# Queries in the rows' product, one gate product of 128 rows, and joined normalisations in a graph-attention kernel

## The chip, the cores and the metric

The kernel runs on one core of a Trainium2 chip. The metric is device time in microseconds for one execution, the median of several runs.

## The reference, cut to what matters

A graph has 6,250 nodes and 200,000 edges sorted by destination. A first network (L0: one attention over the edges and a gate) gives node features of width 64. A second network runs three attention layers with eight heads of eight. One layer, in the reference's words:

```python
h = _ln(x, n1g[l], n1b[l])
q = (h[dst] @ Wq[l] + bq[l]).reshape(-1, H, HD)
kn, ke = h[src] @ Wkn[l] + bkn[l], edge_attr @ Wke[l] + bke[l]     # vn, ve alike
alpha = softmax over the edges of one destination of (q * (kn + ke)).sum(-1) / scale
agg = segment_sum((vn + ve) * alpha, dst)
gate = sigmoid(agg @ Wih[l] + bih[l] + h @ Whh[l] + bhh[l])
upd = agg + gate * (h @ Wself[l] + bself[l] - agg)
x = x + upd @ Wout[l] + bout[l]
x = x + _mlp(_ln(x, n2g[l], n2b[l]), mW1[l], mb1[l], mW2[l], mb2[l])
```

After the third layer x is normalised with a gain and a shift, the input of the three layers is added, and the sum is normalised once more.

## The kernel before

Nodes are sorted by degree into 49 blocks of 128 destinations, one to a partition. All instructions are written out in an order fixed by hand; no scheduler moves them.

**First part, to about 4,850 us.** It sorts, runs L0 over the blocks and computes the edge features (`edge_attr`). Each block ends in `prepare`, described below, which makes what layer 0 needs.

**Layers.** Each of the three layers loops over the blocks in `LORDER` as a pipeline: in iteration i block b is at its keys and values, b1 (the block before) at its softmax and values, b2 at the gate, b3 at the MLP, b4 at preparing the next layer. There are four iterations after the last block, in which the pipeline drains.

- Keys and values of b (`sums`, called once for each group of up to eight edge slots): TensorE multiplies edge features (L1310, float32), then adds rows of neighbours picked by one-hot products. Rows of nodes that stand in the right place come from a table kept in SBUF (L1329, three bfloat16 parts of a row); the others come from rows gathered from HBM (L1317, and L1329 with `g`). ScalarE copies the sums out of PSUM to `b_k` and `b_v` (L1333, L1336). VectorE multiplies `b_k` by the queries and sums over a head (`scores`, L1340 and L1341).
- Gathers: GpSimd issues one indirect DMA per tile of 128 rows (L1239), in bursts of up to twelve into one of four buffers `g`. A burst is issued when TensorE has used the buffer it is to fill.
- Queries of b: one product at the start of the iteration (L1489) into PSUM. The left part of the PSUM tile `b_qe` holds the queries, the right part the exponentials, until the block's values are summed.
- `soft` (L1347 to L1351) and `values` (L1355 to L1380) of b1.
- Small steps of b2, b3, b4 stand in the list `steps` and are put between the groups of b: `turned` transposes the attention of b2 (L559), `gate` multiplies node rows and attention by three matrices (L1390 to L1392; the biases are a 65th row, against a row of ones stored with the node rows `hv`), `gated` mixes on VectorE (L1399 to L1402), `update` multiplies by Wout (L1406, L1407). For b3: `updated` adds and normalises (L1410, `norm`), then `turned2`, `hidden` (L1421) and `close` (L1428 to L1431). In `close`, layers 0 and 1 store x and call `prepare`, which normalises x at once; layer 2 does the two last norms there. For b4 the generator of `prepare` is continued: transpose (L589), the rows' product for keys and values (L601), its copy out (L602) and the split into three bfloat16 parts, stored in the table of the next layer.
- Loads and stores go through the queue of SyncE (SP): node rows and x of the next block at the top of an iteration (`begin`), edge features and one-hots as groups end, stores at the end of an iteration (`flush`).

`norm` is ten VectorE instructions on one block: statistics (L535, L536), variance plus a constant in two scalings (L537), an inverse square root by a bit trick and two Newton steps (`rsqrt`, L519 to L527), and the scaling (L540).


Of the kernel before, what the change touches and what calls it, by code (L numbers as in the profile page):

```python
# [9 lines left out]
F32 = mybir.dt.float32  # L10
# [6 lines left out]
P = 128  # L17
D = 64
# [34 lines left out]
LORDER = (LB, LB - 1) + tuple(b for i in range(24) for b in ((1, 0, *range(2, 24))[i], LB - 2 - i)) [:-1]  # L53
# [371 lines left out]
def passes(ctx, tc, ins, out, meta_d, t0_d, own_d, ident, row_f, ones, norm_c, st_i, id_i, off, end, has, hash_, rdeg,  # L425
# [7 lines left out]
    ht_d = [[dram.tile([D + 1, P], F32, name=f"ht{i}_{b}_d") for b in range(NB)] for i in range(2)]  # L433
    x1_d = [dram.tile([P, D], F32, name=f"x1_{b}_d") for b in range(NB)]
    x2_d = [dram.tile([P, D], F32, name=f"x2_{b}_d") for b in range(NB)]
# [29 lines left out]
    def weights(l):  # L465
# [4 lines left out]
        w["wc"] = wc = lwp.tile([D + 1, 5 * D], F32, name="fwc")  # L470
        bx = lwp.tile([D + 1, 3 * D], F32, name="fbx")
        for i, nm in enumerate(("q", "kn", "vn", "self", "hh")):
            nc.sync.dma_start(wc[:D, i * D : (i + 1) * D], g1("W" + nm))
            nc.sync.dma_start(wc[D : D + 1, i * D : (i + 1) * D], g1("b" + nm).unsqueeze(0))
        for i, nm in enumerate(("ke", "ve", "ih")):
            nc.sync.dma_start(bx[D : D + 1, i * D : (i + 1) * D], g1("b" + nm).unsqueeze(0))
# [4 lines left out]
        w["wih"] = lwp.tile([D, D], F32, name="fwih")  # L481
        nc.sync.dma_start(w["wih"], g1("Wih"))
        w["wout"] = lwp.tile([D, D], F32, name="fwout")
        nc.sync.dma_start(w["wout"], g1("Wout"))
# [17 lines left out]
        nc.vector.tensor_add(wc[D : D + 1, 4 * D :], wc[D : D + 1, 4 * D :], bx[D : D + 1, 2 * D :])  # L502

        nc.vector.tensor_scalar(wc[:, 0:D], wc[:, 0:D], 1.0 / HD ** 0.5, None, ALU.mult)
        nc.vector.tensor_scalar(wc[:, 3 * D : 4 * D], wc[:, 3 * D : 4 * D], 0.5, None, ALU.mult)
# [35 lines left out]

    def norm_twice(wk, once, twice, v):
# [30 lines left out]
    def prepare(wk, mps, w, b, xb, i, hn=None):  # L573
# [9 lines left out]
        kf = wk.tile([P, W1], F32, name="p_kf")  # L583
# [3 lines left out]
        def turned():  # L587
# [4 lines left out]
            stores.append(lambda: nc.sync.dma_start(hd[b][:, :n], ht[:, :n]))  # L592
            if b == 0:
                stores.append(lambda: nc.sync.dma_start(hd[LB][:, LN:P], ht[:, :SPARE]))
# [4 lines left out]
        def rows():  # L599
            pm = mps.tile([P, W1], F32, name="p_pm")  # L600
            nc.tensor.matmul(pm, ht, w["wc"][:, D : 3 * D], start=True, stop=True)  # L601
            nc.scalar.copy(kf, pm)  # L602
            nc.scalar.copy(part[:, 0], kf)
# [1621 lines left out]
```

## Time and profile before

| | |
|---|---|
| runs | 10577.22, 10610.52, 10615.33 us; median 10610.52 |
| profiled execution | 10601.41 us |
| its span, first to last instruction | 10599.5 us |
| mean granted TensorE clock | 0.753 |
| busy: TensorE matmuls, weight loads | 6784.7 us, 4613.5 us |
| busy: VectorE, ScalarE, GpSimd | 5774.5, 3190.8, 3983.4 us |
| gathers of the layers (L1239) | 2,328 in a group of 2245.7 us |
| score products (L1340) | 711 in a group of 542.0 us |

Lines with "PE" are TensorE, "PEld" its weight loads, DVE VectorE, ACT ScalarE, POOL GpSimd. A row of the groups view gives line, engine, operation, output and inputs, shapes and count; then busy time, mean ns of one, and the idle time of the engine before, with what ended it. A row of the timeline gives start, duration, and the instruction; in brackets the idle time of its engine just before and what ended it, where "issue" means that the engine waited for nothing that the trace shows. A row of the waits gives total us, times, longest. A row of busy time by stretch gives the stretch, its length, busy time and count for TensorE matmuls, weight loads, VectorE, ScalarE and GpSimd, then the clock, the DMA engines' share and GB/s.

### The profile page before, as it was taken

To read this page: it belongs to the slowest core of one execution; us is meant where nothing else is said; L and a number is where in the kernel's file an instruction comes from. 1 tells how busy PE (TensorE), PEld (TensorE's weight loads), DVE (VectorE), ACT (ScalarE), POOL (GpSimd) and SP (SyncE) were. 2 spreads that over 40 slices of the span, in tenths; PEclk is the share of its full clock that TensorE was granted. 3 is DMA by queue.
4 is the path that set the end of the run, shared out by engine and by line. 5 is a ranking of instruction groups with operands and counts; after the bars stand their busy time and mean duration, and the time that the engine had idled before them with its cause. 6 is when DMAs were issued, how large, how long until landed. Compare 5 with 4: busy or idle time off the path is not lost.

```text
span 10599.5 us, 163737 instructions
## 1 busy us (share of the span) xinstructions
PE 6784.7 (64%) x62377; PEld 4613.5 (44%) x62377; DVE 5774.5 (54%) x14777; ACT 3190.8 (30%) x6591; POOL 3983.4 (38%) x4201
## 2 busy tenths in 40 slices
PE   2544645555555555576677777677777766677776
PEld 1212222222222222234566666455666655565565
DVE  5544545544555555553556555455665545666666
ACT  1322323322333333342233333223333322222222
POOL 5244333333333333313434444343444434434442
PEclk6676767777777777787787888777778777787877
DMA  4333333333333333334444444444444444444443
GB/s 102 94 89 92 95 89 96 92 90 95 92 91 93 92 91 92 91 87 138 122 128 133 136 136 134 125 123 129 133 134 136 135 130 118 119 126 125 129 127 86
DMA packets 1118549, 1183.96 MB, mean 112 GB/s; under 512 B 669364, under 2 KB 821433, under 8 KB 1110719
## 3 DMA queue, kind: packets, MB, share of 16 engines
q1 hardware_dynamic: 652271, 705.16, 23.3%
q0 software_dynamic: 174624, 393.35, 14.5%
q10 hardware_dynamic: 290864, 74.87, 3.4%
q8 instruction: 502, 8.22, 0.3%
q14 instruction: 288, 2.36, 0.1%
HBM read 936.40 MB, written 236.44 MB: 111 GB/s over the span
## 4 chain that ended last, share of the span: by engine, by line
PE 53%; another core or an unknown queue 19%; issue 17%; ACT 5%; DVE 3%; DMA 1%; POOL 0%; SPq 0%; ACTq 0%; POOLq 0%; DVEq 0%
PE b_pk L1329 18%; PE b_pk L1310 12%; PE f_ph L982 6%; PE b_pk L1317 4%; PE f_tr L945 4%; PE f_pe L964 3%; ACT f_hid L986 2%; ACT s_bc L827 1%; ACT ea L968 1%; PE p_pm L824 1%; ACT f_sq L747 1%; PE p_pm L1421 1%; ACT f_xt L949 1%; PE p_pm L1430 1%
## 5 line engine op out<-in xcount | busy, mean ns | idle before, releaser
L1239 POOL DMA_INDIRECT g<-tab,fidx x2328 | 2245.7, 965 | 3530.2 <-PE b_pk L1317 1720.3
L728 POOL DMA_INDIRECT g<-ft_d,si x1596 | 1522.5, 954 | 2843.0 <-PE e_pt L1045 2370.4
L1329 PE MATMUL b_pk<-ftb,ohl 128*128 128x128 bf16 x21168 | 1889.7, 255 | 881.0 <-issue 830.5
L1329 PEld LDWEIGHTS <-ohl 128*128 128x128 bf16 x21168 | 1592.1, 116 | 1190.5 <-issue 1118.4
L1310 PE MATMUL b_pk<-fwkv,eal 64*128 64x128 f32 x12990 | 1390.8, 316 | 491.0 <-issue 460.2
L1340 DVE TENSOR_TENSOR b_k<-b_k,b_qe 128x768 f32<-128x768 f32 (+6 forms) x711 | 542.0, 762 | 1690.4 <-ACT b_k L1333 1143.9
L964 PE MATMUL f_pe<-f_hid,fw 128*64 128x448 f32 (+4 forms) x2464 | 770.9, 645 | 1080.1 <-ACT ea L968 563.4
L1333 ACT COPY b_k<-b_pk 128x384 f32<-128x384 f32 (+2 forms) x1011 | 475.5, 470 | 3072.4 <-remote 1455.5
L1310 PEld LDWEIGHTS b_pk<-fwkv,eal 64*128 64x128 f32 x12990 | 1064.4, 208 | 719.2 <-issue 634.5
L982 PE MATMUL f_ph<-f_xt,fw 64*128 64x448 f32 (+4 forms) x2464 | 826.1, 678 | 457.8 <-ACT f_xt L949 382.3
L949 ACT ACTIVATE f_xt<-f_tr,feg 128x352 f32<-128x352 f32 (+10 forms) x392 | 253.8, 648 | 2220.2 <-remote 1913.5
L1333 ACT COPY b_v<-b_pk 128x384 f32<-128x384 f32 (+2 forms) x1011 | 872.8, 863 | 0.0
L986 ACT ACTIVATE f_hid<-f_ph,fb 128x448 f32<-128x448 f32 (+4 forms) x1232 | 725.5, 635 | 448.7 <-PE f_ph L982 281.0
L964 PEld LDWEIGHTS f_pe<-f_hid,fw 128*64 128x64 f32 x2464 | 155.1, 149 | 1570.2 <-issue 849.6
L945 PE MATMUL f_tr<-f_mv,f_xs 128*64 128x44 f32 (+10 forms) x12544 | 557.7, 249 | 396.0 <-issue 349.7
L932 DVE TENSOR_TENSOR f_mv<-s_tt,e_fac 128x704 f32<-128x704 f32 (+10 forms) x392 | 349.7, 892 | 778.9 <-remote 663.2
L945 PEld LDWEIGHTS f_tr<-f_mv,f_xs 128*64 128x64 f32 x12544 | 506.3, 160 | 506.1 <-issue 430.4
L982 PEld LDWEIGHTS f_ph<-f_xt,fw 64*128 64x128 f32 x2464 | 261.7, 212 | 822.0 <-ACT f_xt L949 501.2
L1341 DVE TENSOR_REDUCE b_al<-b_k 128x96 f32<-128x768 f32 (+6 forms) x711 | 542.9, 764 | 24.5
L1360 DVE TENSOR_REDUCE b_ag<-b_v 128x64 f32<-128x2816 f32 (+17 forms) x147 | 455.5, 3099 | 5.1
L1359 DVE TENSOR_TENSOR b_v<-b_v,b_qe 128x2816 f32<-128x2816 f32 (+17 forms) x147 | 454.1, 3089 | 0.0
L1317 PE MATMUL b_pk<-g,oh 128*128 128x384 bf16 (+3 forms) x2358 | 446.7, 326 | 0.0
(403 smaller groups left out, 7784.8 us busy)
## 6 DMA issues: line engine op xcount, KB each, us to landing
ohl<-oh_d SPq DMA_DIRECT2D x882, 256.0 KB
eal<-ea_d SPq DMA_DIRECT2D x324, 384.0 KB
oh_d<-s_oh SPq DMA_DIRECT2D x294, 256.0 KB
g<-tab,fidx POOLq DMA_INDIRECT x2328
eal<-ea_d SPq DMA_DIRECT2D x93, 320.0 KB
ea_d<-ea ACTq DMA_DIRECT2D x114, 256.0 KB
eal<-ea_d SPq DMA_DIRECT2D x114, 256.0 KB
ea_d<-ea ACTq DMA_DIRECT2D x130, 224.0 KB
```

The lines of the kernel that those rows point to most:

```text
L728: nc.gpsimd.indirect_dma_start(out=g[:, k - k0, :], out_offset=None, in_=t0_d[:], in_offset=bass.IndirectOffsetOnAxis(ap=got[b]["si"][:, k ...
L945: nc.tensor.matmul(pv[r * D : (r + 1) * D, j], xss[(4 * ORDER.index(b) + 4 * j0 // D) % 4][:, (j0 + j) % (D // 4), :], mv[:, j, :, r::2], ...
L964: nc.tensor.matmul(pe[h * D : (h + 1) * D, :w], w2[:, s, :], hid[s][:, h, :w], start=(s == 0), stop=(s == 1))
L982: nc.tensor.matmul(ph[h][:, :w], w1[r, s * P : (s + 1) * P], xf[r, e0 * D : e1 * D], start=True, stop=True)
L986: nc.scalar.activation(hid[s][:, h, :w], ph[h][:, :w], AF.Relu, bias=b1[:, s : s + 1])
L1239: nc.gpsimd.indirect_dma_start(out=g[:, t - t0, :], out_offset=None, in_=tabs[l % 2][:], in_offset=bass.IndirectOffsetOnAxis(ap=idx[:, f : ...
L1310: nc.tensor.matmul(pk[:, j % 2, j // 2, :], ea[r, e, :], w["wkv"][r], start=(j < 2), stop=False)
L1317: nc.tensor.matmul(pk[:, h, :c, :], ohs[l, b, NW][:, 0, :], rows_[:, slice(t, t + 2 * c - 1, 2), i, :], start=False, stop=(i == 2))
L1329: nc.tensor.matmul(pk[:, h, j, :], o, rows[:, i, :], start=False, stop=(j == c - 1 and q == len(us) - 1 and i == 2))
L1333: nc.scalar.copy(to.rearrange("p (j h) d -> p h j d", h=2), pk[:, :, : n // 2, d0 : d0 + D])
L1340: nc.vector.tensor_tensor(k, k, m["q"].unsqueeze(1).to_broadcast([P, k1 - k0, D]), ALU.mult)
L1341: nc.vector.tensor_reduce(m["al"][:, :, k0:k1].rearrange("p h k -> p k h"), k.rearrange("p k (h d) -> p k h d", h=H), AX.X, ALU.add)
```

## The change

- `prepare` makes queries, keys and values of the next layer in one product of 192 columns and stores the queries beside x (`x1_d`, `x2_d` get 128 columns). `begin` loads both as one tile of SBUF. L1489 goes, and `scores` reads the queries from SBUF instead of PSUM.
- The attention, transposed, is copied to partitions 64 to 127 of the tile whose partitions 0 to 63 are the node rows. One product of 128 rows (Whh over Wih) gives the gate; a second of 64 rows gives Wself. Both outputs lie on PSUM partitions 64 to 127. ScalarE adds the biases: in the Tanh, and in a new Identity that brings the second product to SBUF. VectorE mixes in three instructions instead of four. The row of ones is no longer stored.
- The norm of b3, that of b4 and, in layer 2, the last norm of a fifth block b5 are done together at the top of the iteration (`normed`, `norms`). Before, b3's was there (`updated`) and b4's at the end of `close`. The scaling of layer 2's output is folded into two instructions.
- `steps` has `turned` before b4's transpose, and the gate before b3's transpose.
- `LORDER` begins with four light blocks instead of two, then alternates heavy and light ones as before.

Counted over the program: 294 fewer products on TensorE in the written order, 1,247 fewer instructions on VectorE, 147 more on ScalarE, 150 more DMAs on SP.

```diff
-LORDER = (LB, LB - 1) + tuple(b for i in range(24) for b in ((1, 0, *range(2, 24))[i], LB - 2 - i)) [:-1]
+LORDER = (LB, LB - 1, LB - 2, LB - 3) + tuple(b for i in range(23) for b in ((1, 0, *range(2, 23))[i], LB - 4 - i))[:-1]
...
+    def norms(wk, items):
+
+        k, mvs = len(items), []
+        for v, _ in items:
+            s6 = wk.tile([P, 6], F32, name="n_s6", bufs=4)
+            mvs.append(s6)
+            nc.vector.bn_stats(s6, v)
+        mv = wk.tile([P, k, 2], F32, name=f"n_mv{k}")
+        for j, s6 in enumerate(mvs):
+            nc.vector.bn_aggr(mv[:, j], s6)
+        vv = wk.tile([P, 2, k], F32, name=f"n_vv{k}")
+        for i, f in enumerate((KC, KC * K1 * K1)):
+            nc.vector.tensor_scalar(vv[:, i], mv[:, :, 1], f, f * EPS, ALU.mult, ALU.add)
+        r = rsqrt(wk, vv, k, f"n{k}")
+        for j, (_, put) in enumerate(items):
+            put(mv[:, j, 0:1], r[:, j : j + 1])
...
-            pm = mps.tile([P, W1], F32, name="p_pm")
-            nc.tensor.matmul(pm, ht, w["wc"][:, D : 3 * D], start=True, stop=True)
+            pm = mps.tile([P, 3 * D], F32, name="p_pm")
+            nc.tensor.matmul(pm, ht, w["wc"][:, : 3 * D], start=True, stop=True)
             nc.scalar.copy(kf, pm)
-            nc.scalar.copy(part[:, 0], kf)
+            nc.scalar.copy(part[:, 0], kf[:, D:])
+            stores.append(lambda: nc.sync.dma_start(xd[b][:n, D:], kf[:n, :D]))
...
-            hv = wk.tile([D + 1, P], F32, name="hv", bufs=5)
-            nc.sync.dma_start(hv, ht_d[l % 2][b][:])
-            xb = wk.tile([P, D], F32, name="b_x", bufs=6)
-            nc.sync.dma_start(xb, (x1_d if l == 0 else x2_d)[b][:])
+            hv = wk.tile([P, P], F32, name="hv", bufs=5)
+            nc.sync.dma_start(hv[:D], ht_d[l % 2][b][:])
+            xq = wk.tile([P, 2 * D], F32, name="b_x", bufs=7)
+            nc.sync.dma_start(xq, (x1_d if l == 0 else x2_d)[b][:])
...
-                m["at"] = flip(wk, mps, m["a"], "b_at")
+                pt = mps.tile([D, P], F32, name="p_pm")
+                nc.tensor.transpose(pt, m["a"], ident)
+                nc.scalar.copy(m["hv"][D:], pt)
...
-                nc.tensor.matmul(pg[:, 0], w["wc"][:, 3 * D : 4 * D], hv, start=True, stop=True)
-                nc.tensor.matmul(pg[:, 1], w["wc"][:, 4 * D :], hv, start=True, stop=False)
-                nc.tensor.matmul(pg[:, 1], w["wih"], at, start=False, stop=True)
-                gt = m["gt"] = wk.tile([D, 3, P], F32, name="b_gt")
-                nc.scalar.activation(gt[:, 0], pg[:, 1], AF.Tanh, scale=0.5)
+                nc.tensor.matmul(pg[D:, 1], w["wg"], hv, start=True, stop=True)
+                nc.tensor.matmul(pg[D:, 0], w["wc"][:D, 3 * D :], hv[:D], start=True, stop=True)
+                gt = m["gt"] = wk.tile([P, 4, P], F32, name="b_gt")
+                nc.scalar.activation(gt[D:, 0], pg[D:, 1], AF.Tanh, bias=w["bg"][D:, 0:1], scale=0.5)
+                nc.scalar.activation(gt[D:, 3], pg[D:, 0], AF.Identity, bias=w["bg"][D:, 1:2])
...
-                nc.vector.scalar_tensor_tensor(gt[:, 1], at, 0.5, pg[:, 0], op0=ALU.mult, op1=ALU.add)
-                nc.vector.scalar_tensor_tensor(gt[:, 2], at, -0.5, pg[:, 0], op0=ALU.mult, op1=ALU.add)
-                nc.vector.tensor_mul(gt[:, 2], gt[:, 2], gt[:, 0])
-                nc.vector.tensor_add(gt[:, 1], gt[:, 1], gt[:, 2])
+                nc.vector.scalar_tensor_tensor(gt[:, 1], gt[:, 0], 1.0, gt[:, 3], op0=ALU.add, op1=ALU.mult)
+                nc.vector.scalar_tensor_tensor(gt[:, 2], gt[:, 0], -1.0, at, op0=ALU.add, op1=ALU.mult)
+                nc.vector.scalar_tensor_tensor(gt[:, 1], gt[:, 2], -0.5, gt[:, 1], op0=ALU.mult, op1=ALU.add)
...
-                do(b3, updated)
+                normed(b3, b4, b5 if l == 2 else None)
...
-                    m["q"], m["ex"] = qe[:, :D], qe[:, D : D + c * H].rearrange("p (h k) -> p h k", h=H)
-                    nc.tensor.matmul(m["q"], m["hv"], w["wc"][:, :D], start=True, stop=True)
+                    m["ex"] = qe[:, : c * H].rearrange("p (h k) -> p h k", h=H)
...
-                steps = [lambda: (do(b4, then), do(b2, turned)),
-                         lambda: (do(b3, turned2), do(b2, gate, gated)), lambda: do(b4, more, then),
+                steps = [lambda: (do(b2, turned), do(b4, then)),
+                         lambda: (do(b2, gate, gated), do(b3, turned2)), lambda: do(b4, more, then),
```

## The prediction

> **What bounds the kernel now.** I read the page's totals first, then busy time by stretch, the waits of TensorE, groups by shape, and the timeline of single blocks.
>
> ```profile
> PE 6784.7 (64%) x62377; PEld 4613.5 (44%) x62377; DVE 5774.5 (54%) x14777; ACT 3190.8 (30%) x6591; POOL 3983.4 (38%) x4201
> ```
>
> No engine is full over the span, so the stages count. The three attention layers, which the change edits, run from about 4,850 to 10,570 us. Busy time in the middle of layer 0, then TensorE's waits in all three layers:
>
> ```profile
> 4900.00:6700.00 1800.00, 1366.12 (x13635) 1091.66 (x13632) 1051.66 (x2231) 548.07 (x1284) 712.35 (x737) 0.80 0.47 131
> ```
>
> ```profile
> PE b_pk L1329 <- issue: 852.4, 1151, 2.5
> PE b_pk L1310 <- issue: 460.2, 615, 2.5
> PE p_pm L559 <- DVE b_h L540: 38.9, 9, 10.1
> ...
> PE p_pm L589 <- DVE p_hn L540: 19.7, 8, 2.8
> ```
>
> TensorE is busy 76% of that stretch, and almost all the rest is "issue": 1,313 us in which it waits for no other engine. VectorE makes it wait some 60 us, in 17 places; those I followed lie in the three drains at the layers' ends. The timeline says what goes with "issue":
>
> ```profile
> 5491.48 0.40 PE L1310 MATMUL b_pk<-fwkv,eal 64*128 64x128 f32 x2 [1.04 <-issue]
> ...
> 5492.26 0.95 POOL L1239 DMA_INDIRECT g<-tab,fidx  x1 [0.30 <-issue]
> ...
> 5492.92 0.37 PE L1310 MATMUL b_pk<-fwkv,eal 64*128 64x128 f32 x1 [1.03 <-issue]
> ```
>
> Twelve matmuls of this line otherwise take 0.94 us together; here they come singly. GpSimd's burst of eleven gathers ran from 5485.8 to 5498.2, one each 1.25 us; TensorE slowed from 5489.4 and recovered at 5500.1. Every burst I followed from 5480 to 6010 us shows this: TensorE slows 4 to 6 us after its start and is free about 2 us after its end. The 2,329 gathers form 254 bursts of 2,903 us in all. So a layer is TensorE's own work plus stalls that last as long as gathers do. What shortens TensorE's program shortens the layer; what lengthens a burst lengthens it; what VectorE saves is hidden until the drains.
>
> **The change part by part.**
>
> *Query product (L1489), 147 times.* Removed from the start of each block. On the path, start to start of the next product:
>
> ```profile
> 6786.70 0.30 PEld L1489 LDWEIGHTS b_qe<-fwc,hv 65*128 65x128 f32 x2
> ...
> 6787.07 0.30 PEld L1310 LDWEIGHTS b_pk<-fwkv,eal 64*128 64x128 f32 x4
> ```
>
> 0.37 us; over all blocks the median between the matmuls is 0.365. 147 x 0.365 = −53.7 us. 40 us of stall now also falls on this line; it would fall on the next one, so I don't count it.
>
> *Gate, 147 times.* Three products become two:
>
> ```profile
> 7012.27 0.43 PE L1390 MATMUL p_pm<-hv,fwc 65*64 65x128 f32 x2
> ...
> 7012.54 0.38 PE L1391 MATMUL p_pm<-hv,fwc 65*64 65x128 f32 x2
> ...
> 7012.85 0.43 PE L1392 MATMUL p_pm<-b_at,fwih 64*64 64x128 f32 x2
> ```
>
> The next group starts at 7013.21: steps of 0.27, 0.31 and 0.36 us. One goes; I take the middle, 147 x 0.31 = −46 us (−40 to −53). A rule speaks against this. The Trainium skill (TensorEngine Tiling (Array Packing), Key Properties) says that a change of tiling mode drains TensorE, and the new products write PSUM partitions 64 to 127, a column placement that no row here has. The three steps differ by 0.09 us although the last one changes the row count, so a drain looks like at most that. By the row the gate gives −46; with two more such drains per block (147 x 0.18 = +26) −20. I take the row and keep −20.
>
> *Rows' product (L601), 147 times, 49 of them before the layers.* 128 columns become 192. From L1489 (64 columns) to L601 (128), the interval goes from 0.365 to 0.370 us, so width has cost nothing; half of a 64-row, 128-column pass in L1310's groups (0.87 us for 12, so 0.073 each) for each of two passes bounds it at 0.075. I take 0.04: 147 x 0.04 = +6 us (0 to 11). The wider ScalarE copy (L602, 0.31 us) gains perhaps 0.06, beside other work: ScalarE is busy 30%.
>
> *ScalarE, gate.* One Identity more per block, about L1394's 0.27 us: 40 us of an engine idle 69% of the layers; it delays the next PSUM copies, of which there are two buffers, and TensorE waits some 24 us for those copies now. On the path 0 (0 to +10).
>
> *VectorE.* A norm is ten instructions, 2.43 us from 6702.20 to 6704.63. Two together are sixteen: by the two-wide rows (0.16 us each) and 0.03 between, 3.6 us for 4.9. The gate's four become three (0.28 each). In the steady blocks this is worth nothing. But both norms move to the top of the iteration, behind the softmax's subtraction, and the transposes of the first two steps wait for them. TensorE's L589 starts 8.6 us or more after L1410 in three of four blocks and 5.7 in the tenth percentile; 3.6 us fits in. Behind the norms stands the value product, 0.6 us later in layers 0 and 1, which a block two steps later uses: covered.
>
> *Drains.* There, nothing covers a norm. One iteration takes 11.6 us (L1410 from 6701.95 to 6713.55) with two norms in its loop; joined, −2 us twice in each of layers 0 and 1. In layer 2 it takes 13.55 us (10558.46 to 10572.01) with three norms; joined, −4 us twice. −16 us (−6 to −25).
>
> *Queries in SBUF.* The score product L1340 now reads two SBUF operands. Its own time stays:
>
> ```profile
> L1340 DVE TENSOR_TENSOR b_k<-b_k,b_qe 128x320 f32<-128x320 f32 x61 | 29.7, 486 | 179.3 <-ACT b_k L1336 116.7 <-issue 61.9 <-ACT b_hid L1423 0.7
> ...
> L1350 DVE TENSOR_TENSOR b_al<-b_al,b_md 128x320 f32<-128x320 f32 x15 | 7.4, 491 | 0.5
> ```
>
> 486 ns with one operand in PSUM, 491 with both in SBUF. But gathers feel it:
>
> ```profile
> 5297.12 0.57 DVE L1347 TENSOR_TENSOR b_al<-b_al,fam 128x400 f32<-128x400 f32 x1
> 5297.22 1.29 POOL L1239 DMA_INDIRECT g<-tab,fidx  x1 [0.30 <-issue]
> ...
> 5298.82 0.95 POOL L1239 DMA_INDIRECT g<-tab,fidx  x1 [0.30 <-issue]
> ```
>
> The gather that started inside L1347 took 1.29 instead of 0.95 us: it ended 0.82 us after L1347 did. The long gathers that I followed all fit "0.13 us after its start a gather waits for such an instruction's end"; laid over the whole timeline this gives 46 us for L1347 and L1350, where all gathers together are 53 us longer than 0.953 each. None is longer than 1.0 us with only L1340 or L1359, which have a PSUM operand. Laying L1340's 715 intervals under the same rule: 115 gathers would wait, 0.32 us each, +37 us, and a burst's delay is a stall's delay. Here the skill's rule is harsher (SBUF — State Buffer, "SBUF: two separate sides"): VectorE with two SBUF inputs and a GpSimd instruction that reads SBUF exclude each other for the whole instruction. L1350 beside gathers never lengthened (491 to 493 ns at 320 columns), so the whole gather isn't covered. By the row +37; if each of the 364 score products that overlap a gather delayed it for its whole 0.61 us, +224. I take 37 (0 to 224).
>
> *Transfers.* 150 query stores and 256 B more in each row of 147 loads, on queues that keep the DMA engines 47% busy; the block load is issued an iteration ahead. The query stores join the flush behind a ScalarE copy, as the stores beside them do. 0 (−5 to +10). *Block order*: the four lightest blocks first. The first four gathers are 6+8+9+10 = 33 instead of 6+8+10+10 = 34; the total is the same. 0 (±15).
>
> **Sum** against the profiled execution's 10601.4: −53.7 −46 +6 −16 +37 = −73, so 10,528. The median shown is 9 us above that execution: 10,610 − 73 = 10,537, say 10,540 us, −0.66%.
>
> **Rivals.** (A) *The lock eats the gain.* At +80 to +120 us instead of +37 the sum is −30 to +10: about 10,595. For it: scores run just as gathers start. Against: the intervals laid out give 37. (B) *TensorE's gain doesn't reach the end*: if bursts pace the layers, a shorter program only waits longer for the next one. Then −16 + 37: about 10,630. For it: the stalls end with bursts. Against: 1,720 us of gather waiting are for L1317, so TensorE starts the bursts. (C) *Slower*: the score products, one mechanism, hold the gathers for nearly their full length. From +37 + 73 = 110 us of delay the gain is gone, from 163 it is slower by over 0.5%; at 224, 10,610 + 114 = about 10,725. Against it: no such length shows for L1347.
>
> **How the numbers follow.** The likeliest case has 0.55 and by itself 10,490 to 10,585. A 0.17, B 0.12, C 0.16. 0.5% is 53 us, about what a measurement of this kernel can tell from no change. Of the likeliest, 0.05 lies within it and 0.50 below 10,557; A, B and that 0.05 make 0.34 within; C 0.16. The range takes in A, B and the near part of C, and below, the best ends of gate, drains and order: 10,480 to 10,660.
>
> **What would show it.** Right: L1489 gone; the gate's two products in 0.6 us; L1340's successor within 2% of its time; gathers of 1.2 to 1.8 us where they start inside it, some 90 us over 0.953 each in all; drains shorter by 2 and 4 us per iteration. Wrong: gathers far longer than that, gate steps above 0.45 us, or TensorE waiting for norms outside the drains.

## The result, and the profile after

The changed kernel took 10,620.9 us (median of 20 runs, 10,590.9 to 10,630.5), the kernel before on the same chip 10,600.5 us (20 runs): ratio 1.0016, 95% interval [1.001, 1.0023]. So nothing was gained, and about 20 us were lost, where the forecast was 73 us faster. The time lies in the forecast's range and outside its likeliest case. The profiled execution has a span of 10,598.6 us, against 10,599.5 before.

The kernel before took 10,518 to 10,600 us (medians) in four of the six sets of runs made together, the result's among them ("with stalls" below), and 6,885 and 6,889 us in the other two ("without stalls"), and as one chip gave 10,518 us in one set and 6,885 us in a later one, this is a condition and not a property of a chip. Ratios are always to the kernel before in the same set. Across sets with stalls I compare them to about 0.1%, an estimate from one pair: the unedited change gave 1.0016 and 1.0027.

The totals of the profile after, busy time in the middle of layer 0, and TensorE's waits in the layers:

```profile
PE 6688.1 (63%) x61789; PEld 4462.2 (42%) x61789; DVE 5411.2 (51%) x13681; ACT 3350.5 (32%) x6738; POOL 4021.6 (38%) x4201
```

```profile
4900.00:6700.00 1800.00, 1330.01 (x13418) 1045.17 (x13419) 952.40 (x1962) 597.26 (x1317) 724.45 (x737) 0.79 0.47 132
```

```profile
PE b_pk L1356 <- issue: 1264.6, 1624, 2.6
...
PE b_pk L1337 <- issue: 199.5, 309, 4.9
...
PE p_pm L613 <- DVE p_hn L1437: 29.4, 8, 5.6
```

TensorE is busy 97 us less (6784.7 before) and VectorE 363 us less (5774.5), with 1,096 instructions fewer in the profile (14,777 before, 13,681 after) and not the 1,247 of the count above. But TensorE's "issue" waits on the two lines of keys and values (L1356 was L1329, L1337 was L1310) add up to 1,464 us, where they were 1,313. The work went, and waiting took its place.

To see this without the classes of waits, I took from each trace the steps from one product's start on TensorE to the next, in the three stretches from a layer's first exponential to its last (the drains lie outside them). A step over 0.5 us is called long.

| kernel | stretches, us | short steps, us | long steps, us |
|---|---|---|---|
| before | 5,448 | 3,565 | 1,886 |
| after | 5,456 | 3,487 | 1,976 |

Short steps lost 78 us, long ones gained 90. (A second trace of the same changed kernel, in experiment 2, has 3,434 and 2,004 us, so the split into the two is good to some 50 us.) The first part (first exponential of layer 0 at 4,890.0 and 4,894.6 us) and the drains do not hide anything: the drains went from 102.0, 101.9 and 57.6 us to 98.9, 99.9 and 48.9, together −13.8.

The gathers, and the score product in its commonest shape, before and then after:

```profile
L1239 POOL DMA_INDIRECT g<-tab,fidx x2328 | 2245.7, 965 | 3530.2 <-PE b_pk L1317 1720.3 <-issue 632.2 <-PE p_pm L1406 455.8
...
L1340 DVE TENSOR_TENSOR b_k<-b_k,b_qe 128x768 f32<-128x768 f32 x312 | 297.4, 953 | 754.8 <-ACT b_k L1333 754.1
```

```profile
L1266 POOL DMA_INDIRECT g<-tab,fidx x2328 | 2283.1, 981 | 3501.5 <-PE b_pk L1344 1761.4 <-issue 635.0 <-PE p_pm L1433 450.7
...
L1367 DVE TENSOR_TENSOR b_k<-b_k,b_x 128x768 f32<-128x768 f32 x312 | 298.7, 957 | 803.6 <-ACT b_k L1360 766.2 <-DMA eal<-ea_d 32.5 <-DMA fbx<-in_L_gnn_bve_dram 4.5
```

The gathers took 37.4 us more in all. The score product has two operands in SBUF now and takes 957 ns where it took 953.

The gate in one block:

```profile
7055.29 0.43 PE L1419 MATMUL p_pm<-hv,fwg 128*64 128x128 f32 x2
7055.65 0.43 PE L1420 MATMUL p_pm<-hv,fwc 64*64 64x128 f32 x2
7056.01 0.30 PE L583 MATMUL p_pm<-fident,b_h 128*64 128x128 f32 x1
```

Its two products take 0.72 us from the first one's start to the start of what follows (median of 147); the three took 0.94. The rows' product, with 192 columns, takes 0.474 us in the same way where it took 0.370.

### The profile page after: what moved, and what is told of

It is laid out like the page before. It is cut to its first block, busy times and chain, and to the rows that moved or that the text cites. A ratio compares the mean times of both kernels' runs of the same rounds, so it can differ in the third digit from the quotient of the medians.

```text
span 10598.6 us, 161843 instructions
## 1 busy us (share of the span) xinstructions
PE 6688.1 (63%) x61789; PEld 4462.2 (42%) x61789; DVE 5411.2 (51%) x13681; ACT 3350.5 (32%) x6738; POOL 4021.6 (38%) x4201
## 5 line engine op out<-in xcount | busy, mean ns | idle before, releaser
L1266 POOL DMA_INDIRECT g<-tab,fidx x2328 | 2283.1, 981 | 3501.5 <-PE b_pk L1344 1761.4
L1356 PE MATMUL b_pk<-ftb,ohl 128*128 128x128 bf16 x21168 | 1957.3, 253 | 1280.9 <-issue 1243.4
L1356 PEld LDWEIGHTS <-ohl 128*128 128x128 bf16 x21168 | 1569.1, 114 | 1663.1 <-issue 1611.8
L1367 DVE TENSOR_TENSOR b_k<-b_k,b_x 128x768 f32<-128x768 f32 (+9 forms) x711 | 545.3, 767 | 2094.5 <-ACT b_k L1360 1270.2
L1337 PE MATMUL b_pk<-fwkv,eal 64*128 64x128 f32 x12990 | 1317.8, 318 | 237.4 <-issue 199.5
L1337 PEld LDWEIGHTS b_pk<-fwkv,eal 64*128 64x128 f32 x12990 | 1034.9, 212 | 429.5 <-issue 346.5
L1368 DVE TENSOR_REDUCE b_al<-b_k 128x96 f32<-128x768 f32 (+9 forms) x711 | 542.9, 764 | 24.5
```

The costliest lines, as they stand in the source:

```text
L1266: nc.gpsimd.indirect_dma_start(out=g[:, t - t0, :], out_offset=None, in_=tabs[l % 2][:], in_offset=bass.IndirectOffsetOnAxis(ap=idx[:, f : ...
L1337: nc.tensor.matmul(pk[:, j % 2, j // 2, :], ea[r, e, :], w["wkv"][r], start=(j < 2), stop=False)
L1356: nc.tensor.matmul(pk[:, h, j, :], o, rows[:, i, :], start=False, stop=(j == c - 1 and q == len(us) - 1 and i == 2))
L1367: nc.vector.tensor_tensor(k, k, m["q"].unsqueeze(1).to_broadcast([P, k1 - k0, D]), ALU.mult)
L1368: nc.vector.tensor_reduce(m["al"][:, :, k0:k1].rearrange("p h k -> p k h"), k.rearrange("p k (h d) -> p k h d", h=H), AX.X, ALU.add)
```

## The experiments

### 1. Four variants, without stalls

All four fell into the condition without stalls. They say little on the forecast's own case, and much on the condition. The first copies the queries to PSUM, so that a score product has one operand there again; the second is the change with the old block order; the third the kernel before with its query product three times; the fourth the kernel before with the new order.

```diff
+                    nc.scalar.copy(qe[:, :D], m["q"])
+                    m["q"], m["ex"] = qe[:, :D], qe[:, D : D + c * H].rearrange("p (h k) -> p h k", h=H)
-                    m["ex"] = qe[:, : c * H].rearrange("p (h k) -> p h k", h=H)
```

> The changed kernel, but ScalarE copies each block's queries from SBUF to the PSUM tile that held them before, so the score products read one PSUM operand again and no gather waits for them. Lock theory (the gathers' delay costs more than the 37 us counted): 60 to 100 us faster than the changed kernel, about 10,540 us. Absorption theory (TensorE's shorter program does not reach the end): only the gathers' own 37 us, 20 to 40 us faster, about 10,585. Order theory (the new order of the blocks costs): the same 37 us, about 10,585. In all, gathers lie back at 0.95 us.

> The changed kernel with the old order of the blocks. Order theory: 50 to 80 us faster than the changed kernel, about 10,555 us. Lock and absorption theories: within 15 us of the changed kernel, about 10,620.

```diff
-                    nc.tensor.matmul(m["q"], m["hv"], w["wc"][:, :D], start=True, stop=True)
+                    for _ in range(3):
+                        nc.tensor.matmul(m["q"], m["hv"], w["wc"][:, :D], start=True, stop=True)
```

> The kernel before, with each block's query product issued three times in a row to the same place. It adds two products of 0.365 us in each of 147 blocks, 107 us of TensorE work. The sum of the prediction and the lock theory: 95 to 120 us slower than before, about 10,705 us. Absorption theory: less than half of it, 10,610 to 10,650.

> The kernel before with the new order of the blocks and nothing else. Order theory: 50 to 80 us slower than before, about 10,665 us. Lock and absorption theories: within 15 us of before, about 10,600.

Measured, the kernel before at 6,889.3 us: queries in PSUM 6,550.6, ratio 0.9511 [0.9496, 0.9526]; old order 6,588.4, 0.9566 [0.9553, 0.9579]; query product three times 6,878.8, 0.998 [0.9973, 0.9987]; new order in the kernel before 6,889.8, 1.0002 [0.9994, 1.001]. So the change, with one of its edits undone, is worth 4.3 to 4.9% here. No theory had expected this. TensorE's clock by slice, in the result's run of the change and in the variant with queries in PSUM:

```profile
PEclk6776777776777777787777777777777777777777
```

```profile
PEclk6678999898889998999899999989999999999998
```

VectorE's waits for L1367 in the same two runs, the result's first:

```profile
DVE b_k L1367 <- ACT b_k L1360: 1270.2, 452, 49.5
...
DVE b_k L1367 <- issue: 559.3, 126, 20.4
```

```profile
DVE b_k L1367 <- ACT b_k L1360: 172.9, 108, 38.4
...
DVE b_k L1367 <- issue: 3.4, 5, 0.9
```

And busy time in layer 0 of the variant with queries in PSUM:

```profile
3200.00:4200.00 1000.00, 978.16 (x12711) 815.45 (x12712) 891.54 (x1848) 570.89 (x1301) 683.77 (x710) 0.99 0.76 229
```

TensorE is busy 98% and VectorE 89%, at a granted clock of 0.99 where the other condition has 0.79. The long steps are 133 us, not 1,976, although the gathers themselves take as long: 2240.6 us in their group. The short steps are 3,070 us, not 3,487; so of the 2,260 us that the stretches are shorter here, some 420 can go with the clock and 1,843 are long steps. VectorE's "issue" waits vanish too, so what gathers hold up in the other condition is not TensorE alone.

The traces say more of it. They hold the times at which each engine's semaphore was raised, the signal by which another engine learns that an instruction is done. I call a signal late when its semaphore is not raised until more than 0.3 us after the instruction's end. In the layers of the kernel before, with stalls, 1,233 of the 1,623 signals of TensorE that fall into a burst of gathers or the 2 us behind it are late, and 4 of the 2,319 others. ScalarE's (514 of 1,242, and 9 of 1,860) and VectorE's (2,453 of 4,985, and 32 of 1,928) are late in the same way. Without stalls, in the kernel before with the new order, 83 of 3,310 of TensorE's are. So in the condition with stalls the engines hear late of each other's work while gathers are issued. Whether TensorE's slow starts come from that, and what sets the condition, is not shown.

In the kernel before, TensorE is busy 95% and VectorE 91% in layers 0 and 1 here (the fourth kernel's trace), and that the query product three times is no slower tells that TensorE alone was not the limit. But most of the gain lies in layer 2. From the fourth kernel's trace to the first's, the stretches of the three layers fall by 46, 48 and 239 us, of 349 us in all. Waits in layer 2 of the fourth kernel, then of the first:

```profile
ACT b_qe L1351 <- DVE b_al L1350: 352.0, 48, 8.8
...
PE b_pk L1310 <- ACT b_v L1333: 167.1, 46, 14.6
```

```profile
ACT b_qe L1378 <- DVE b_al L1377: 147.4, 44, 5.2
...
PE b_pk L1337 <- ACT b_v L1360: 35.6, 28, 11.0
```

In layer 2 the kernel before has the two last norms of `close` on VectorE ahead of the block's last scores and its softmax. ScalarE's exponential waits for the softmax, its copies out of PSUM stand behind the exponential, and TensorE waits for the copies. The change takes those norms away from there. With stalls, TensorE's waits for these copies of `b_v` are 3.4 us in layer 2 before the change and 4.6 after it, so there is nothing of this to win. The edit of the norms was not undone by itself in this condition, so its share of the 239 us is not measured.

### 2. The changed kernel again, queries in PSUM, gathers in threes, two more products

Made together, with stalls. The kernel before took 10,544.4 us.

> The changed kernel, unedited, beside the kernel before on one chip, for the runs sent with it. Two conditions have been seen: one in which the kernel before takes about 10,600 us and TensorE's starts fall to one in 0.7 us while gathers run, and one in which it takes 6,889 us without these stalls. Where there are stalls: ratio 1.000 to 1.004 again. Where there are none: TensorE and VectorE are nearly full in the layers, the change takes some 360 us from VectorE's list and 97 us from TensorE's, and with the new order and the queries in SBUF it should lie between the two variants already run there (0.951 and 0.957): 0.950 to 0.957.

> The changed kernel with the queries copied to PSUM, so that the score product has one operand there as before. Theory A (the gathers that wait for score products with two operands in SBUF eat the gain): gathers of the layers about 37 us shorter in all than in the changed kernel; where gathers stall TensorE the stalls shrink by about as much and the time is 30 to 60 us under the changed kernel. Theory B (bursts of gathers pace the layers and TensorE's gain is waited away): gathers shorter by the same 37 us, time within 20 us of the changed kernel where there are stalls. Without stalls: within 25 us of the changed kernel by both.

For the threes, a buffer's gathers are put into a list, and behind each group of products this follows:

```diff
+                    drip(3, m["v"][:, 0, u1 - 2 : u1])
...
+        def drip(n, after=None):
+            if due and after is not None:
+                nc.gpsimd.tensor_copy(pace, after)
+            for l, b, g, t0, t in due[:n]:
+                f = TFIRST[b] + t
+                nc.gpsimd.indirect_dma_start(...)
+            del due[:n]
```

> The changed kernel with its gathers in threes: behind each group of products GpSimd copies two numbers of that group's values and then issues three gathers, in place of a whole burst of up to twelve when a buffer comes free. The number of gathers and all other work are the same. If a stall begins only some 5 us after a burst has begun, a burst of three (some 3.5 us) should end before it: stalls of the three layers from 2,300 us to under 1,000, and the time, where there are stalls, lower by 800 to 1,500 us. If a gather slows TensorE whenever it runs, the stalls only change their places: within 100 us. If TensorE starves because the issue of gathers itself is late (buffers filled later): slower by up to 300 us. Without stalls: within 40 us of the changed kernel.

```diff
+                    for _ in range(2):
+                        nc.tensor.matmul(qe[:, :D], m["hv"][:D], w["wc"][:D, :D], start=True, stop=True)
```

> The changed kernel with two more products of the size of the old query product at each block's start, which nothing reads: 294 products, 0.365 us each by the steps of the first trace, so +107 us for TensorE. If a layer is TensorE's work plus stalls (the prediction's sum): slower than the changed kernel by 90 to 110 us where there are stalls. If the bursts pace the layers (theory B): 0 to 30 us. Without stalls, TensorE is busy 97% in the layers of the variants run there and VectorE 92%, so 60 to 107 us slower; near 0 if VectorE sets the pace.

| kernel | time, us | ratio | short steps | long steps |
|---|---|---|---|---|
| the change | 10,577.1 | 1.0027 [1.0018, 1.0037] | 3,434 | 2,004 |
| queries in PSUM | 10,543.6 | 1.0001 [0.9993, 1.0009] | 3,470 | 1,935 |
| gathers in threes | 10,124.7 | 0.960 [0.9586, 0.9614] | 3,381 | 1,639 |
| two more products | 10,599.1 | 1.0048 [1.0034, 1.0062] | 3,514 | 1,959 |

*Queries in PSUM.* 33 us under the change, and the gathers shorter by 21.5 us in their group:

```profile
L1266 POOL DMA_INDIRECT g<-tab,fidx x2328 | 2250.7, 967 | 3474.0 <-PE b_pk L1344 1718.6 <-issue 632.2 <-PE p_pm L1433 450.7
```

In the result's trace, 98 gathers have a score product still running 0.13 us after their start; 72 of them are longer than 1.1 us. With the queries in PSUM there are 98 such gathers too, and none is longer. So the second SBUF operand is the cause. The forecast's +37 us is +33 in time here.

*Threes.* 452 us under the change, the best version of this condition. Gathers less than 1.5 us apart count as one burst here, and a long step counts to the burst in which, or in the 2 us behind which, it begins. Bursts of up to 3.5 us (128 of them) now hold 0.24 us of TensorE's long steps each, bursts of 12 to 30 us (112 that came about because several threes followed each other) 11.8 us. So a short burst ends before the stall begins. The gain fell below the 800 us expected because only part of the gathers came apart.

*Two more products.* The totals of the change in this set, then with the two products:

```profile
PE 6663.7 (63%) x61789; PEld 4412.8 (42%) x61789; DVE 5411.7 (51%) x13681; ACT 3347.1 (32%) x6738; POOL 4012.7 (38%) x4201
```

```profile
PE 6754.9 (64%) x62377; PEld 4506.4 (43%) x62377; DVE 5412.5 (51%) x13681; ACT 3347.0 (32%) x6738; POOL 4012.1 (38%) x4201
```

TensorE is busy 91 us more, and the time rises by 22 (4 to 40, an estimate from the intervals of the two ratios); the stretches in the two traces differ by 36. The sum's own rule would have said 107. So added work of TensorE reaches the end only in part here; theory B's number held.

### 3. Gathers in fours, with the change and without it, and the old order

Made together, with stalls. The kernel before took 10,518.0 us. Here four gathers follow each of the four groups of products with rows from SBUF, and none follow the other groups:

```diff
+                    if kind != "o":
+                        drip(len([x for x in due if x[:2] == (l, b) and x[3] <= part[4]]))
                     sums(m, part, u0, u1)
+                    if kind == "o":
+                        drip(4, m["v"][:, 0, u1 - 2 : u1])
```

> The changed kernel with its gathers in fours: behind each of the four groups of products with rows from SBUF in a block, GpSimd copies two columns of that group's values and then issues four gathers; a buffer's gathers are no longer issued all together. Number of gathers and other work as before. From the run with threes: bursts of 3.5 to 6 us cost TensorE 0.5 us each and bursts of 12 to 30 us over 9 us; there half of the gathers still came in long bursts, and the time fell by 452 us. If that reading is right, with all gathers in fours (some 580 bursts of 4 to 5 us, 0.5 us of slow starts each) TensorE's slow starts fall from some 1,750 to under 500 us, and where gathers stall TensorE the time is 900 to 1,300 us below the changed kernel: ratio to the kernel before 0.88 to 0.92. If the recovery after a burst needs more time than there is between two bursts: 0.94 to 0.97. Where there are no stalls: 0.945 to 0.96, as the change alone.

> The kernel of fours with the queries copied to PSUM. Where gathers stall TensorE, theory A (a gather waits for a score product with two operands in SBUF) says gathers some 30 us shorter in all; with bursts too short to stall, this should now be worth less than the 33 us it was worth before: 0 to 25 us below the kernel of fours. Where there are no stalls: within 20 us.

> The kernel before with its gathers in fours in the same way. Theory B (the change's gain is waited away because bursts stall TensorE) says that without the stalls the change is worth what it saves on the engine that then sets the pace: the kernel of fours with the change should be 150 to 350 us faster than this one (on a chip without stalls the change brought 300 to 340 us). If the change is worth nothing for another reason, the two are within 40 us. Against the kernel before, where there are stalls: 0.90 to 0.94; where there are none: 0.99 to 1.01.

> The changed kernel with the old block order. The change shortened TensorE's own work by 97 us and its drains by 14, of which a fifth should reach the end by the run with two more products (22 of 107 us); with +33 us for the gathers that wait this leaves -1 us, and +20 to +33 was measured. Theory O: the rest is the new order, under which bursts merge (254 before, 218 to 236 after); then the old order gives 235 to 260 bursts and a time 20 to 40 us under the changed kernel, where there are stalls. If the order is not the cause: within 10 us of the changed kernel. Where there are no stalls the old order was 38 us slower than the variant with queries in PSUM: ratio 0.955 to 0.958.

With the change 10,283.2 us, 0.9774 [0.976, 0.9787]; with queries in PSUM as well 10,278.2, 0.9775 [0.9758, 0.9791], 5 us less and within the 0 to 25 expected; without the change 10,416.1, 0.9904 [0.9889, 0.9919]. The change with the old order and its bursts whole: 10,579.8, 1.0059 [1.0046, 1.0073].

The fours missed their expectation. GpSimd's timeline in the first of them:

```profile
5410.60 0.20 POOL L1270 COPY pace<-b_v 128x2 f32<-128x2 f32 x1 [6.51 <-ACT b_v L1370]
5411.26 0.98 POOL L1273 DMA_INDIRECT g<-tab,fidx  x1 [0.46 <-issue]
...
5415.07 0.96 POOL L1273 DMA_INDIRECT g<-tab,fidx  x1 [0.30 <-issue]
5416.03 0.19 POOL L1270 COPY pace<-b_v 128x2 f32<-128x2 f32 x1
5416.38 0.98 POOL L1273 DMA_INDIRECT g<-tab,fidx  x1 [0.16 <-issue]
```

The second group of a part was copied out at 5411.6 to 5412.4 us, while the first four gathers ran, so two fours follow each other: 250 bursts last 8 to 12 us, and hold 4.9 us of long steps each, counted as for the threes. The stalls are thus not gone, and what theory B says of a kernel without them was not tested. Even so, the change is worth 133 us between these two kernels, where it was worth nothing with whole bursts. By layers this is 0 in layer 0, +8 in layer 1, −128 in layer 2, and −17 in the drains. Layer 2 is the place told of under experiment 1: TensorE's waits there for ScalarE's copies are 170.5 us in the fours without the change and 19.9 with it. It is less than the 150 to 350 us expected by theory B, and the two kernels differ in their bursts too: 121 bursts of at most four gathers without the change, 22 with it.

The old order is slower, not faster, by 0.3 to 0.4% of the time against the change's two ratios: the new order helps by 34 to 45 us where bursts are whole, by ratios across sets, and theory O falls. The stretches in the traces do not show this gain: 5,450 us with the old order, 5,456 and 5,430 with the new one.

### 4. Pauses ahead of the bursts, query product three times, and the old order of steps

Made together, and without stalls. The kernel before took 6,885.2 us.

```diff
+                for _ in range(n):
+                    nc.gpsimd.memset(pace, 0.0)
```

> The changed kernel with eight memsets of GpSimd (some 4 us together) ahead of each burst of gathers, but for the four at a layer's start, so that no burst follows another without a gap. Theory M (bursts that follow each other without a gap cost TensorE its recovery between them, 2 to 4 us for each such pair): pairs without a gap from some 25 to 45 to under 10, TensorE's slow starts 60 to 120 us less, and the time 40 to 110 us under the changed kernel, ratio to the kernel before 0.990 to 0.998. If the gaps don't matter: within 15 us of the changed kernel, or slower by up to 100 us where a later burst makes TensorE wait for its rows. Where gathers don't stall TensorE: the same or up to 60 us slower.

> The kernel before with the same pauses. It has 7 pairs of bursts without a gap, so theory M gives it less than the changed kernel: 0 to 40 us faster (110 pairs have a gap of some 2 us, which grows to 6). If a longer gap is itself what helps TensorE, it gains as much as the changed kernel does: 40 to 110 us. If later bursts cost: slower.

> The kernel before with its query product three times in place of once: 294 more products, +107 us of TensorE's work at the starts of the blocks. The prediction's sum: +107 us, ratio 1.010. Theory B (most of such work disappears in the time in which TensorE would wait anyway; two more products cost the changed kernel 22 us): 0 to +30 us, ratio 1.000 to 1.003. Where gathers don't stall TensorE: 0.998 again.

> The changed kernel with the small steps in the old order: b4's transpose before that of b2, b3's transpose before the gate. Theory S: this order makes bursts meet; with the old one the pairs without a gap fall towards 7, and the time falls by 20 to 60 us against the changed kernel (ratio to the kernel before 0.997 to 1.001). If the order of the steps doesn't matter: 1.0016 to 1.0027 again.

The pauses cost 10.3% with the change (7,594.5 us, 1.1032 [1.1016, 1.1048]) and 8.7% without it (7,484.8, 1.0871 [1.0853, 1.0889]): GpSimd became late, and TensorE waited for gathered rows.

```profile
PE b_pk L1348 <- DMA g<-tab,fidx: 422.5, 123, 10.1
```

The query product three times gave 0.9974 [0.9961, 0.9988], the old order of steps 0.9569 [0.9556, 0.9582]. None of the four tells on theories M, B and S, which are about stalls; they repeat that the change is worth over 4% here, and show what a pause would cost.

### 5. A shorter pause, and each norm by itself

Made together, with stalls. The kernel before took 10,531.8 us. The pause is five memsets in place of eight. The other kernel does the norms one by one at the place where the change has them:

```diff
-                if items:
-                    norms(wk, items)
+                for one in items:
+                    norms(wk, [one])
```

> The changed kernel with five memsets of GpSimd (some 2.5 us) ahead of each burst of gathers but for the four at a layer's start. Where gathers stall TensorE: theory M (bursts that meet cost TensorE 2 to 4 us each) says pairs without a gap under 10, slow starts of TensorE 50 to 120 us less, and a time 30 to 110 us under the changed kernel (ratio 0.991 to 0.999). If meeting bursts don't matter: within 15 us of it, or slower by up to 100 us. Where gathers don't stall TensorE, four pauses of 4 us cost about 1,040 us because GpSimd became the bound; 2.5 us then costs 300 to 700 us.

> The changed kernel with the normalisations where the change puts them, but each done by itself: VectorE has some 150 to 190 us more to do in the layers. The prediction (VectorE's saving is hidden outside the drains): where gathers stall TensorE, 0 to 20 us slower than the changed kernel, from the drains alone. Where they don't stall it and VectorE is busy 92% in the layers: 100 to 190 us slower than the changed kernel, ratio 0.965 to 0.982.

With pauses 10,362.8 us, 0.9848 [0.9826, 0.987], which is 1.7 to 1.8% under the change, some 190 us; the expectation's best was 110. GpSimd's timeline shows where they act:

```profile
5922.28 2.87 POOL L1265 MEMSET pace<- 128x512 f32 x5
5925.34 0.99 POOL L1270 DMA_INDIRECT g<-tab,fidx  x1 [0.18 <-issue]
...
5935.14 2.88 POOL L1265 MEMSET pace<- 128x512 f32 x5
5948.10 0.96 POOL L1270 DMA_INDIRECT g<-tab,fidx  x1 [10.08 <-PE b_pk L1348]
```

Before a burst that has to wait for TensorE anyway (the second), the memsets lie in the waiting time. Only a burst that would follow the last one within a few us (the first) is put off. There are 117 of those among 255 (the five bursts at each layer's start are left out), in each of the traces with whole bursts and stalls. Their gap to the burst before them, from the last gather's end to the first gather's start:

| kernel | sum of 117 gaps, us | gaps under 1.5 us | long steps, us | stretches, us |
|---|---|---|---|---|
| before | 264 | 7 | 1,886 | 5,448 |
| after (the result) | 205 | 25 | 1,976 | 5,456 |
| the change, in 2 | 171 | 43 | 2,004 | 5,430 |
| queries in PSUM, in 2 | 218 | 23 | 1,935 | 5,398 |
| two more products, in 2 | 178 | 39 | 1,959 | 5,466 |
| old order, in 3 | 163 | 47 | 2,026 | 5,450 |
| each norm by itself | 172 | 42 | 2,022 | 5,461 |
| short pause | 362 | 0 | 1,643 | 5,250 |

Against the change in 2, the pause adds 191 us of gaps and takes 180 us from the stretches: longer gaps gave back about their own length. What the gaps are worth was tried by this one run. The table also shows how far two traces of one program differ: the unedited change has 205 us and 25 short gaps in the result's trace, 171 and 43 in that of 2.

Each norm by itself: 10,625.8 us, 1.0092 [1.0078, 1.0105], which is 0.65 to 0.76% over the change, 70 to 80 us. The drains (103.8, 103.5, 55.0) give 14 of them against the result's trace. By the ratios, then, VectorE's saving counts inside the layers too; the stretches in the traces show only a part of it, 5,461 us against 5,456 and 5,430.

## Why the prediction was wrong

**What held.** *Query product, gate, rows' product*: the forecast was −94 us for TensorE, and its busy time fell by 97. By starts it is less: the gate gave 147 x 0.22 = −32 us, short of the −46 and inside −20 to −53, and the rows' product 147 x 0.104 = +15, above its range of 0 to 11. With the query product that is −54 −32 +15 = −71. *Queries in SBUF*: +37 forecast; +33 in time and 21 to 37 in the gathers. That a gather waits only for an instruction that is still running 0.13 us after its start held for 72 of 98. (The check behind it was misread: before, all gathers together are 27 us longer than 0.953 each, not 53, and those that the rule points at beside L1347 and L1350 are 25 us longer, not 46. The gathers are 2,328, and their 254 bursts last 2,878 us; the burst from 5485.8 us has ten. None of this moves the sum.) The Trainium skill's page "SBUF — State Buffer" (section "SBUF: two separate sides") says that a VectorE instruction with two inputs in SBUF and a GpSimd instruction that reads SBUF exclude each other for the whole instruction; read as covering the whole gather that would have been 224 us, and the trace decides against that. *Drains*: −16 forecast, −13.8 measured. *Change of tiling mode*: the gate's two steps are 0.36 us each, where the three were 0.27, 0.31 and 0.36; two more drains of 0.09 us would have left a gain of 0.13 per block, and 0.22 was measured.

**The step that failed** is the rule under the sum: "What shortens TensorE's program shortens the layer". TensorE's own work fell about as forecast, and its long steps grew by 90 us in its place; two products added per block, 107 us by the rule, cost 22. The rule counts in full what reaches the end only in part. Two readings under it were wrong.

First, I argued against rival B that "TensorE starts the bursts", from the 1,720 us of gather waiting for L1317. Every burst does wait for TensorE's signal that its buffer is free, but in two ways. In 138 of 255 bursts the signal stands 0.01 us (median) behind the end of the matmul that gives it. In the other 117 that matmul had ended before the burst ahead did, and the signal stands 7.3 us behind it before the change, 7.2 after; in 109 of the 117 before, and 99 after, the burst starts within 0.35 us of the signal. Most of those bursts start when a late signal comes, and not when TensorE's work is done. They stood 2.26 us apart (median) before, and after the change 1.86, with 25 in place of 7 standing less than 1.5 apart. Such a pair of bursts before the change, the last gather of the one and the first of the other:

```profile
5999.43 0.95 POOL L1239 DMA_INDIRECT g<-tab,fidx  x1 [0.30 <-issue]
6002.44 0.95 POOL L1239 DMA_INDIRECT g<-tab,fidx  x1 [2.06 <-remote]
```

"remote" stands where the trace finds no instruction whose end fits the signal; here TensorE's semaphore was raised at 6002.18 to 6002.26 us. A closer pair in the profile after, GpSimd and then TensorE:

```profile
5965.54 0.95 POOL L1266 DMA_INDIRECT g<-tab,fidx  x1 [0.30 <-issue]
5967.87 0.95 POOL L1266 DMA_INDIRECT g<-tab,fidx  x1 [1.37 <-remote]
```

```profile
5966.89 0.26 PE L1356 MATMUL b_pk<-ftb,ohl 128*128 128x128 bf16 x1 [0.98 <-issue]
...
5975.55 0.37 PE L1356 MATMUL b_pk<-ftb,ohl 128*128 128x128 bf16 x2 [1.02 <-issue]
5976.97 0.37 PE L1356 MATMUL b_pk<-ftb,ohl 128*128 128x128 bf16 x2 [1.05 <-issue]
5979.10 0.37 PE L1356 MATMUL b_pk<-ftb,ohl 128*128 128x128 bf16 x2 [1.76 <-issue]
5979.40 2.08 PE L1337 MATMUL b_pk<-fwkv,eal 64*128 64x128 f32 x12
```

One burst ends, the next begins before TensorE has recovered, and TensorE stays slow from 5961.2 to 5979.4 us, across both. The sum had a term for how long gathers are, and none for how far apart bursts stand. By the gaps, 59 us were lost from before to after; at 0.94 us each (180/191, from the pause) that is 55 us. With TensorE's −71, the drains' −14 and 33 for the queries, the sum is +3, against −1 between the two profiled spans and +20 between the medians. So the missing term has the right size, but that it is the cause is not shown: it is priced by one run, two traces of the same change differ by 34 us in it, and with the queries in PSUM 47 us of gaps came back together with 33 us of time in all, so the term for the gathers and that for the gaps overlap.

Second, "what VectorE saves is hidden until the drains": by the ratios, the joined norms are worth 70 to 80 us in place of 16. The order, taken as 0 ± 15, is worth 34 to 45 us. Both are gains that the forecast did not have, and the sum just made has no line for them. They can act through the gaps as well as by themselves, so they are not to be added to it.

**What stays open.** With two more products the time rose by 22 us and not by 107, and the gaps don't explain that. The gains of the norms and of the order, added to the rest, would not give the measured time: undone one at a time, the edits don't add up here. Which edit brings the bursts closer was not found: with the old order, with each norm by itself, or with more products, 39 to 47 gaps stay short, and with the queries in PSUM 23, but the unedited change has 25 and 43 in its two traces. The old order of the small steps was run only without stalls; the gate, with its new Identity on ScalarE, and the wider stores and loads were not undone by themselves.

**The rivals.** A (10,595): the wait of gathers is real, but cost the 33 us that the forecast had counted, and not +80 to +120. B (10,630) named the nearest time, and the two extra products bear it out; its place, the bursts, was right. That its number came so near is in part luck, as it had no gain for the norms and the order. C did not occur. The likeliest case missed because the failing step was the rule of its sum and not one of the terms to which a range was given.

## What to carry to other kernels

Where instructions on an engine come singly while another engine issues gathers, count the bursts and the gaps between them and not only their total length: short bursts and a gap of a few microseconds can be worth more than the work saved (here, with stalls, 1.7% for a pause on an engine that is not the bottleneck, 4% for gathers in threes). Ask of each burst what releases it, and when the releasing work had ended: of these waits for TensorE, 117 in 255 were for a signal that came some 7 us late, and not for work. And a saving should be priced in the condition in which it is measured: the same change cost 0.2 to 0.3% in one and, but for an edit, gained over 4% in the other.

## What the runs showed of the hardware

- The same program ran in 10,518 to 10,600 or in 6,885 us, with the same gathers (965 and 957 ns each in the kernel before and its new order). In the slower condition TensorE's steps during a burst of gathers come in multiples of about 0.71 us: in the timeline above 1.42 from 5975.55 to 5976.97, and 2.13 to 5979.10. A stall begins about 5 us after its burst and ends 1.7 to 2 us after it (medians of the traces). I did not find what sets the condition.
- In that condition three in four of TensorE's signals come over 0.3 us late during a burst (1,233 of 1,623), and next to none outside (4 of 2,319); without stalls 83 of 3,310 are late during bursts.
- VectorE has, with the change, 559 us of "issue" waits for the score products there and 3 us in the other condition (the queries in PSUM), so the hold-up is not TensorE's own.
- Of the versions run, gathers in threes are the fastest with stalls (0.960), and they beat both kernels; without stalls it is the change with queries in PSUM (0.951). The threes were not run without stalls, where pauses on GpSimd cost 9 to 10%, so no version is shown to be best in both.
